# A sparse graph network's set-up: adjacency tiles fetched at once, keys spread by identity matmuls, three ranks on ScalarE, projections and slots spaced anew

## The chip, the cores and the metric

The kernel runs on one core of one Trainium2 chip. A core has TensorE (PE; its weight loads are PEld), VectorE (DVE), ScalarE (ACT), GpSimd (POOL) and SyncE (SP, which here only issues DMAs). Each engine takes its own instructions in the order in which the program has them and waits on semaphores for the others. Times are microseconds of the device (us), from one launch of the whole kernel.

## The reference

Four layers of graph network run one after another on 16 graphs of 1024 nodes with 128 features, which all share one adjacency matrix; each of its entries is 1 with a chance of 0.0078125, about 8 neighbours a node. Layers 0, 2 and 3 are attention layers with 8 heads, layer 1 has one additive score for each pair of nodes.

```python
def _L0_gnn_ref(adj_matrix, h, Wq, Wk, Wv, Wo, ...):   # layers 2 and 3 are the same
    Q = (h @ Wq).reshape(B, N, NUM_HEADS, HEAD_DIM)
    K = (h @ Wk).reshape(B, N, NUM_HEADS, HEAD_DIM)
    V = (h @ Wv).reshape(B, N, NUM_HEADS, HEAD_DIM)
    scores = jnp.einsum('bnhd,bmhd->bhnm', Q, K) / jnp.sqrt(...)
    scores = jnp.where(mask, -jnp.inf, scores)          # mask: adj_matrix == 0
    attn = jax.nn.softmax(scores, axis=-1)
    attn_out = jnp.einsum('bhnm,bmhd->bnhd', attn, V).reshape(B, N, OUT_DIM)
    x = _layer_norm(h + (attn_out @ Wo + bo), ln1_g, ln1_b)
    y = jax.nn.relu(x @ W1 + b1) @ W2 + b2
    return _layer_norm(x + y, ln2_g, ln2_b)

x = L0(adj, x); x = L1(x, adj); x = L2(adj, x); x = L3(adj, x)
```

## The kernel before, in words

The kernel does not multiply by the dense mask. It finds each node's neighbours once, and then fetches only the neighbours' rows of keys and values from tables in DRAM by indirect DMA.

**Set-up, `graph` (L227).** It counts the degree of each node (L256, one count over a 128 x 1024 tile of the adjacency for each of T = 8 tiles), makes a key from degree and node number (L298), and ranks the nodes by it: the keys are spread over all partitions as a 128 x 1024 block in PSUM (`over_partitions`, L282: transpose on PE, copy on DVE, eight matmuls against the selector `sel`), and each rank is the count of keys that are greater (L302, eight compares on DVE). From the ranks come one-hot rows (`perm`, L335), whose matmuls (L344) put node numbers into sorted order (L354). With those, the adjacency rows are gathered again in sorted order (`by_position`, L362, on POOL's queue) into the three buffers `edges`, and for each of eight groups of rows DVE finds the neighbours with MAX8 and MATCH_REPLACE8 (L395 to L403) and writes them to `lists`.

**Slots, `slots` (L408).** For each unit of 128 sorted nodes the lists are spread by PE (L413, `spread`), and some thirty small DVE instructions (L427 to L463) turn them into row indices `idx` and 0/1 matrices `marks`. Unit 0's come at the room "slots" of the set-up, those of the others during the first seven units.

**The first projections, `at_once` (L810).** Eight times, for 128 nodes of the first eight graphs: an x tile is loaded (L816), transposed on PE (L646) and copied by ACT (L652), multiplied by the weights of keys and values (L576), copied by ACT (L580) and written to the table of layer 0 by SP (L585). One such projection is four steps of a generator. What `graph` yields says how many steps are taken there: a number is that many steps, a string calls for something else ("load", "spread", "queries", "slots"; L1128 to L1144). So the yields fix where the projections stand between the other instructions of PE, ACT and SP. The projections of the other eight graphs, `at_leisure` (L787), run later between the parts of the first units.

**The body (L1160 to L1227).** There are 64 units: 4 layers, 2 groups of 8 graphs, 8 tiles of nodes. A unit is a handful of parts of two neighbour rows for each node. A part is gathered on POOL's queue (`gathered`, L929, four buffers `e` of the pool `gathers`, four parts ahead), multiplied by the queries `qr` (L958), reduced to scores (L981), put through the exponential (ACT, L985), weighted (L1009) and summed over neighbours by matmuls against `marks` (L1025). Between the parts, `others` (L1099) takes steps of the tails of the unit before (output projection, norms, feed-forward), of the fronts (the next slots and queries) and of the projections at leisure, one front step to a call.

The order is written out by hand (`manual_schedule`): each engine runs its instructions as the generators emit them. The four gather buffers `wide` serve as scratch in the set-up and are zeroed by POOL (L240, L248, L1155), because rows that a bounds check leaves out keep what was there.

## Time and profile before

| | us |
|---|---|
| median of three timed runs | 2261.7 |
| lowest and highest of them | 2255.61, 2262.03 |
| the profiled execution, whole | 2254.23 |
| its span, first to last instruction | 2251.9 |
| PE busy in the span | 2043.1 |
| DVE busy | 1872.9 |
| ACT busy | 1528.3 |
| POOL busy | 1016.3 |

How to read it: the span is one execution taken by the hardware's profiler, and the times further on are counted from its start. A timeline lists the instructions of one engine with start, duration, line, operation, what is written and read with its size, how often, and in square brackets the idle time just before with what ended it. "DMA to landing" is the time from a DMA's issue until its data is there. The granted TensorE clock is 0.962 of full speed on the mean.

Three more lines of the timelines place ACT and POOL in the set-up. The first two are the copies that begin the second and third projection; the last shows how POOL zeroes three gather buffers.

```profile
17.08 1.07 ACT L652 COPY xT<-ps 128x512 f32<-128x512 f32 x2
...
21.97 1.07 ACT L652 COPY xT<-ps 128x512 f32<-128x512 f32 x2
```

```profile
8.95 10.66 POOL L248 MEMSET e<- 128x4128 f32 x3
```

### The profile page before, as it was taken

Reading aid. Unit: us, or ns where it says so; the run is one execution under the profiler, and the core shown is the slowest. Engines: PE = TensorE matmul, PEld = TensorE weight load, DVE = VectorE, ACT = ScalarE, POOL = GpSimd, SP = SyncE. Lnnn points to the kernel's source line nnn. Section 1 sums busy time; section 2 is a strip of 40 time slices with the busy share of each in tenths; the row PEclk is TensorE's granted clock in tenths of the full one; section 3 lists DMA queues with packets and bytes.
Section 4 is the critical chain, followed back from the end, with each engine's and each line's share of the span. In section 5 each row is a group of like instructions: output and inputs, shape, how many; then the busy total and the mean of one; then the engine's idle time right before and its main releaser. Section 6 shows DMA issues by size and latency. Waiting matters only on the chain.

```text
span 2251.9 us, 36507 instructions
## 1 busy us (share of the span) xinstructions
PE 2043.1 (91%) x13140; PEld 1271.3 (56%) x13140; DVE 1872.9 (83%) x1472; ACT 1528.3 (68%) x5041; POOL 1016.3 (45%) x699
## 2 busy tenths in 40 slices
PE   6589999899999999998999989999999998998986
PEld 5456665555555555554556655656655555555554
DVE  7897899888887577768988889989798998888893
ACT  3346777777777655555677777777777777676765
POOL 3343445354435368884343434334444544453540
PEclk8799999999999999999999999999999998999999
DMA  7897877778788699997997978887888788687860
GB/s 254 290 323 275 298 272 279 268 263 289 284 296 272 221 341 356 360 358 291 327 329 268 318 260 302 303 313 276 284 282 305 265 286 279 225 279 271 288 227 21
DMA packets 164700, 636.05 MB, mean 282 GB/s; under 512 B 34568, under 2 KB 37384, under 8 KB 116014
## 3 DMA queue, kind: packets, MB, share of 16 engines
q0 software_dynamic: 88720, 485.08, 61.0%
q1 hardware_dynamic: 75792, 148.57, 19.1%
q8 instruction: 105, 1.72, 0.3%
q14 instruction: 83, 0.68, 0.1%
HBM read 581.08 MB, written 92.34 MB: 299 GB/s over the span
## 4 chain that ended last, share of the span: by engine, by line
PE 41%; ACT 18%; issue 16%; DVE 11%; DMA 9%; POOL 5%; POOLq 0%; DVEq 0%; ACTq 0%
PE acc L1025 9%; DMA e<-table,idx 8%; PE yps L746 5%; PE ps L576 4%; POOL e L946 4%; PE ps L646 4%; ACT qr L912 4%; PE ps L732 3%; PE ps L909 3%; DVE pr L958 3%; ACT z L624 3%; DVE sc L981 3%; DVE pr L1009 2%; PE yps L750 2%; ACT z L639 2%
## 5 line engine op out<-in xcount | busy, mean ns | idle before, releaser
L946 POOL DMA_INDIRECT e<-table,idx x576 | 854.1, 1483 | 1101.8 <-DVE pr L1009 902.1
L1009 DVE TENSOR_TENSOR pr<-e,ex 128x2048 f32<-128x2048 f32 (+1 forms) x320 | 661.6, 2076 | 46.7 <-ACT ex L985 24.9
L958 DVE TENSOR_TENSOR pr<-e,qr 128x2048 f32<-128x2048 f32 x192 | 441.6, 2300 | 132.7 <-PE acc L1025 55.7
L1025 PE MATMUL acc<-pr,marks 128*32 128x512 f32 x2624 | 519.1, 608 | 14.8 <-DVE pr L1009 10.8
L981 DVE TENSOR_REDUCE sc<-pr 128x128 f32<-128x2048 f32 (+1 forms) x240 | 497.5, 2073 | 8.0
L624 ACT ACTIVATE z<-yps,root 128x128 f32<-128x128 f32 x888 | 317.5, 388 | 35.7 <-PE yps L765 17.2
L1025 PEld LDWEIGHTS acc<-pr,marks 128*32 128x32 f32 x2624 | 107.7, 110 | 269.4 <-issue 226.7
L639 ACT ACTIVATE z<-yps,rstd 128x128 f32<-128x128 f32 x888 | 254.0, 369 | 7.2
L746 PE MATMUL yps<-W,f 128*128 128x128 f32 x1520 | 251.8, 283 | 7.3 <-ACT f L741 1.8
L741 ACT ACTIVATE f<-ps,b 128x512 f32<-128x512 f32 x190 | 129.8, 695 | 157.6 <-PE ps L732 157.2
L746 PEld LDWEIGHTS yps<-W,f 128*128 128x128 f32 x1520 | 205.0, 192 | 51.0 <-issue 25.6
L576 PE MATMUL ps<-Wkv,xT 128*128 128x256 f32 x768 | 215.0, 419 | 20.0 <-ACT xT L652 16.7
L912 ACT COPY qr<-ps 128x512 f32<-128x512 f32 x384 | 197.3, 600 | 40.6 <-PE ps L909 40.5
L909 PE MATMUL ps<-q,rep 32*128 32x512 f32 x768 | 175.3, 661 | 34.7 <-ACT q L904 33.5
L732 PE MATMUL ps<-x,W 128*128 128x512 f32 x384 | 190.4, 620 | 12.5 <-ACT x L654 12.5
L624 ACT ACTIVATION_READ_ACCUMULATOR z<-yps,root 128x1 f32 x888 | 201.7, 227 | 0.0
L646 PE MATMUL ps<-ident,z 128*128 128x128 f32 x896 | 177.5, 299 | 25.5 <-ACT z L639 20.7
L646 PEld LDWEIGHTS ps<-ident,z 128*128 128x128 f32 x896 | 115.2, 142 | 149.2 <-ACT z L639 72.1
L580 ACT COPY kv<-ps 128x512 f32<-128x512 f32 x176 | 103.2, 589 | 131.9 <-PE ps L576 119.4
L576 PEld LDWEIGHTS ps<-Wkv,xT 128*128 128x128 f32 x768 | 146.5, 205 | 76.4 <-ACT xT L652 21.1
L721 PE MATMUL yps<-Wo,oT 128*128 128x128 f32 x768 | 160.3, 292 | 8.6 <-ACT oT L652 8.5
L722 PE MATMUL yps<-centre,x 128*128 128x128 f32 x768 | 155.5, 285 | 3.6
(176 smaller groups left out, 2597.7 us busy)
## 6 DMA issues: line engine op xcount, KB each, us to landing
table<-kv SPq DMA_DIRECT2D x88, 512.0 KB, 6.5
kept<-xT SPq DMA_DIRECT2D x96, 256.0 KB, 5.4
x<-kept SPq DMA_DIRECT2D x48, 512.0 KB, 9.2
qx<-qr SPq DMA_DIRECT2D x48, 256.0 KB, 6.7
e<-table,idx POOLq DMA_INDIRECT x576, 8.1
table<-kv SPq DMA_DIRECT2D x32, 256.0 KB, 7.7
qx<-qr SPq DMA_DIRECT2D x18, 384.0 KB, 9.1
qx<-qr SPq DMA_DIRECT2D x42, 128.0 KB, 8.1
```

Source lines behind the costliest of these rows:

```text
L576: nc.tensor.matmul(ps[:, k, :], x[:, i + k, :], w[LAYERS[l][0], "Wkv"], start=True, stop=True,)
L624: nc.scalar.activation(z[:, i, :], y[:, i, :], AF.Square, scale=D**-0.5, bias=root, accum_out=total[:, i : i + 1],)
L639: nc.scalar.activation(z[:, i, :], y[:, i, :], AF.Copy, scale=rstd[:, i : i + 1])
L646: nc.tensor.transpose(ps[:, i, :], z[:, i, :], ident)
L732: nc.tensor.matmul(ps, p["W1"][:, f * P : (f + 1) * P], x1.rearrange("p g n -> p (g n)"), start=True, stop=True,)
L746: nc.tensor.matmul(ps[:, i, :], f1[:, f, i * P : (i + 1) * P], p["W2"][:, f, :], start=(f == 0), stop=False,)
L912: nc.scalar.copy(qs[u][:, j, h * GH * D : (h + 1) * GH * D], pss[j])
L946: nc.gpsimd.indirect_dma_start(out=es[i][:, k, :], out_offset=None, in_=tables[l, g][:, :], in_offset=bass.IndirectOffsetOnAxis(ap=idx[:, ...
L958: nc.vector.tensor_tensor(prs[i][0][:, :n, :], es[i][:, :n, :ROW], qx[u].rearrange("p (o c) -> p o c", o=1) if (MIX, 0) in piece else of_p ...
L981: nc.vector.tensor_reduce(sc[:, :n, :], prs[i][0][:, :n, :].rearrange("p k (a d) -> p k a d", d=HD), mybir.AxisListType.X, ALU.add,)
L1009: nc.vector.tensor_tensor(prs[i][k0 // 2][:, :m, :].rearrange("p k (a d) -> p k a d", d=d), es[i][:, k0 : k0 + m, base : base + ROW].rearr ...
L1025: nc.tensor.matmul(outs[32 * j : 32 * j + 32], marks[:, mark, :], rhss, start=(chunk == mine[0]), stop=(chunk == mine[-1]),)
```

## The change

- All eight adjacency tiles are fetched first, straight into the empty gather buffers `wide[0]` and `wide[2]`, instead of three at a time through `edges`. The buffers are zeroed afterwards: `wide[0]` by POOL, `wide[2]` by a copy on ACT; of `wide[1]` only the last columns are zeroed.
- `over_partitions` has no transpose, no copy and no selector: a column of the key, repeated 128 times, is the stationary operand of a matmul with the identity.
- Of the eight compares for the ranks, three become `Sign` activations with a sum on ACT (the sum s gives the rank as (s + 1023) / 2), five stay on DVE.
- The steps of `at_once` are taken elsewhere: none during the degree counts, five and two more around the ranks, one at every second one-hot row, six after the sorted nodes, three at each MAX8.
- `slots` has one more empty step between the spread and the DVE work of units 1 to 7, so five steps a unit are handed to the fronts instead of four.

```diff
+SIGNS = 3
...
-        ahead = [by_columns(t) for t in range(3)]
+        held = [wide[k][:, m * N : (m + 1) * N].bitcast(I32) for k in (0, 2) for m in range(T // 2)]
+        for t in range(T):
+            nc.sync.dma_start(held[t], a["adj"][t * P : (t + 1) * P, :])
         yield 0
...
-        junk = wide[1][:, :N]
-        sel = wide[1][:T, N : 2 * N].rearrange("k (t n) -> k t n", n=P)
-
-        nc.gpsimd.memset(wide[1], 0.0)
+        junk, other = wide[1][:, :N], wide[1][:, N : 2 * N]
...
-        for e in wide[3:] + wide[:1] + wide[2:3]:
-            nc.gpsimd.memset(e, 0.0)
+        nc.gpsimd.memset(wide[1][:, 3 * N :], 0.0)
...
             nc.vector.tensor_scalar(
-                junk, ahead[t], 0.0, 0.0, ALU.not_equal, ALU.add, accum_out=deg[:, t : t + 1]
-            )
-            if t + 3 < T:
-                ahead.append(by_columns(t + 3))
-            if t == 4:
+                junk, held[t], 0.0, 0.0, ALU.not_equal, ALU.add, accum_out=deg[:, t : t + 1]
+            )
+            if t == 0:
...
-            yield 1 + t // 4
+            yield 0
...
-            ps = bank([T, P])
-            nc.tensor.transpose(ps, col, ident)
-            turn = s1.tile([T, P], F32, tag="turn", name="turn")
-            nc.vector.tensor_copy(turn, ps)
             dst = accs.tile([P, HF, GH * D], F32, tag="acc", name="acc")
             dst = dst.rearrange("p h d -> p (h d)")
             for t in range(T):
                 nc.tensor.matmul(
-                    dst[:, t * P : (t + 1) * P], sel[:, t, :], turn, start=True, stop=True
+                    dst[:, t * P : (t + 1) * P], col[:, t : t + 1].to_broadcast([P, P]), ident,
+                    start=True, stop=True,
                 )
...
-        for t in range(T):
+        ahead_of = s1.tile([P, T], F32, name="ahead_of")
+        nc.vector.tensor_scalar(ahead_of, key, -1.0, None, ALU.mult)
+        nc.gpsimd.memset(wide[0], 0.0)
+        for t in range(T - SIGNS, T):
+            nc.scalar.activation(
+                other, keys, AF.Sign, bias=ahead_of[:, t : t + 1], accum_out=rank[:, t : t + 1]
+            )
+        nc.scalar.copy(wide[2], seen[:, 0, :1].to_broadcast(list(wide[2].shape)))
+        for t in range(T - SIGNS):
             nc.vector.tensor_scalar(
                 junk, keys, key[:, t : t + 1], 0.0, ALU.is_gt, ALU.add,
                 accum_out=rank[:, t : t + 1],
             )
             yield 1
+        yield 2
+        nc.vector.tensor_scalar(
+            rank[:, T - SIGNS :], rank[:, T - SIGNS :], 0.5, (N - 1) / 2, ALU.mult, ALU.add
+        )
...
                 spread = over_partitions(pack)
                 nc.scalar.copy(values, spread)
-            yield 0
+            yield t % 2
...
         nc.vector.tensor_tensor(bad, bad, low, ALU.add)
-        yield 2
+        yield 6
...
                     nc.vector.match_replace(v, lists[:, q, k : k + 8], last, 0.0)
-                yield 1
+                yield 3
...
             if q:
+                yield
                 yield
                 yield
...
-        fronts.extend([islice(rest, 4), second] + more)
+        fronts.extend([islice(rest, 5), second] + more)
...
-                        fronts.append(islice(rest, 4))
+                        fronts.append(islice(rest, 5))
```

More of the change, by code (lines that the diff above doesn't have):

```diff
@@ L227, in graph @@
     def graph(wide):
-        def by_columns(t):
-            return fetch_edges(
-                lambda e: nc.sync.dma_start(e, a["adj"][t * P : (t + 1) * P, :])
-            )
-        ahead = [by_columns(t) for t in range(3)]
+        held = [wide[k][:, m * N : (m + 1) * N].bitcast(I32) for k in (0, 2) for m in range(T // 2)]
+        for t in range(T):
+            nc.sync.dma_start(held[t], a["adj"][t * P : (t + 1) * P, :])
         yield 0
         iota, values, vs = wide[3][:, :N], wide[3][:, N : 2 * N], wide[3][:, 2 * N : 4 * N]
-        junk = wide[1][:, :N]
-        sel = wide[1][:T, N : 2 * N].rearrange("k (t n) -> k t n", n=P)
-        nc.gpsimd.memset(wide[1], 0.0)
+        junk, other = wide[1][:, :N], wide[1][:, N : 2 * N]
         whole = wide[1][:, 2 * N : 3 * N].bitcast(I32)
@@ L266, in graph @@
                     nid, cols[:, 1, :], float(P), cols[:, 0, :], ALU.mult, ALU.add
-                )
-                nc.vector.tensor_copy(
-                    sel,
-                    ident[:T, :T].rearrange("k (t o) -> k t o", o=1).to_broadcast([T, T, P]),
                 )
```

## The prediction

> **What bounds the kernel now.** I read the page first, then the timelines of the engines over the first 140 us, because `graph`, `slots` and `at_once` run only there, and last the waits between 100 and 480 us, where the spaced slots act.
>
> ```profile
> PE   6589999899999999998999989999999998998986
> ...
> DVE  7897899888887577768988889989798998888893
> ACT  3346777777777655555677777777777777676765
> ...
> PEclk8799999999999999999999999999999998999999
> ```
>
> Each digit is a slice of 56 us. PE is at nine tenths almost everywhere except the first two slices. So the long body is bound by PE; a change to the set-up can only move the body as a whole, earlier or later, by the time at which the first gathers start.
>
> What sets that time is VectorE's chain (DVE; start, duration, then idle before and its releaser):
>
> ```profile
> 12.68 1.22 DVE L256 TENSOR_SCALAR_CACHE_REDUCE e<-edges 128x1024 f32<-128x1024 int32 x1
> ...
> 30.44 0.16 DVE L298 SCALAR_TENSOR_TENSOR key<-deg,nid 128x8 f32<-128x8 f32 x1
> ...
> 35.34 1.28 DVE L302 TENSOR_SCALAR_CACHE_REDUCE e<-acc,key 128x1024 f32<-128x1024 f32 x1 [3.94 <-PE acc L291]
> ...
> 48.31 0.75 DVE L335 TENSOR_SCALAR perm<-e,rank 128x1024 bf16<-128x1024 f32 x1
> ...
> 55.04 0.18 DVE L354 COPY sorted<-ps 128x24 f32<-128x24 f32 x1 [0.47 <-PE ps L344]
> ...
> 61.60 1.23 DVE L395 SCALAR_TENSOR_TENSOR e<-edges,e 128x1024 f32<-128x1024 int32 x1 [2.78 <-DMA edges<-in_adj,node_i]
> ...
> 88.96 0.18 DVE L449 TENSOR_SCALAR idx<-little 128x24 int32<-128x24 int32 x1
> ...
> 98.86 2.29 DVE L958 TENSOR_TENSOR pr<-e,qr 128x2048 f32<-128x2048 f32 x1 [0.67 <-DMA e<-table,idx]
> ```
>
> The reader is to see the milestones: degrees from 12.68, the key at 30.44, first rank 35.34, first one-hot row (`perm`) 48.31, the sorted nodes at 55.04, the first list at 61.60 (after waiting for the gathered adjacency rows), the indices of unit 0 at 88.96 + 0.18, the first product at 98.86. Beside it runs the table of layer 0, which the first gather also reads:
>
> ```profile
> 61.75 0.51 SPq L585 DMA_DIRECT2D table<-qx  x1
> ...
> 82.66 0.51 SPq L585 DMA_DIRECT2D table<-qx  x1
> ```
>
> ```profile
> 55.92 1.12 POOL L363 DMA_INDIRECT edges<-in_adj,node_i  x1 [36.32 <-DVE node_i L359]
> ...
> 89.48 1.01 POOL L946 DMA_INDIRECT e<-table,idx  x1 [4.06 <-DVE little L452]
> 90.79 1.95 POOL L946 DMA_INDIRECT e<-table,idx  x1 [0.30 <-issue]
> ```
>
> The last table write is issued at 82.66, and the first row gather at 89.48 is released by DVE. So the two paths end close together: lists at 89.1, table within some 6 us of 83.2 (landings of table writes: 3.4/6.9/12.1 us least, median, most). DMA over the same stretch, by windows (the last two numbers: DMA share, GB/s):
>
> ```profile
> 15.00:30.00 15.00, 10.73 (x56) 8.81 (x54) 8.89 (x20) 8.08 (x15) 4.61 (x2) 1.00 1.01 354
> ...
> 42.00:50.00 8.00, 5.85 (x39) 4.52 (x37) 7.05 (x18) 4.41 (x8) 0.00 (x0) 1.00 0.92 314
> ...
> 62.00:76.00 14.00, 6.59 (x32) 5.33 (x32) 13.65 (x15) 5.20 (x10) 3.06 (x4) 0.85 0.80 281
> 76.00:90.00 14.00, 10.42 (x52) 7.66 (x56) 13.38 (x29) 5.58 (x10) 4.02 (x5) 0.79 0.77 248
> ```
>
> A full share (1.01) is 354 GB/s here.
>
> **What the Trainium skill says.** "TensorE: Matmul & The Clock Gate", section Step-by-step: matmuls stay in program order and only weight loads are pulled ahead. The trace agrees: at 69.1 PE stands 8.4 us (77.52) for a loaded x, with the last four projections behind it. "ScalarE: Activation LUTs", section What ACT_TABLE_LOAD costs: an activation with a bias pointer takes about 280 ns + 0.833 ns an element. The trace agrees: L624 at 128 elements is 388 ns, the copy L350 of 1024 is 1.01 us. "SBUF — State Buffer", section SBUF: two separate sides: VectorE's two-port modes and GpSimd lock each other out for whole instructions. It agrees: four small `rep` copies took 10.73 us beside POOL's MEMSETs, and the degree count at 12.68 took its usual 1.22 us beside them. "DMA: Bandwidth & Descriptors", section Specifications, gives about 358 GB/s from HBM for a core; the 354 above is that.
>
> **The change, step by step.**
>
> *Degrees.* Before, only three adjacency tiles were in flight: DVE waited 1.10 + 2.46 + 2.48 = 6.0 us for tiles, and did not start before 12.68 because of the locked copies. Now eight tiles (4.2 MB, 12 us at 354 GB/s, so all by about 15) go out first. POOL's early work shrinks from four MEMSETs of 3.53 us to one of 1056 columns (about 0.9 by width) and ends near 6.5. DVE takes tile 0 when it lands (0.76 + 5.5 = 6.3), 1.26 us; the small ops (L155 to L278) about 3.2; seven more counts 8.8; key at about 20.2 against 30.44: **10 us earlier**. The first three x tiles are now issued behind the adjacency, at no cost since no projection starts before 32. The MEMSET of `wide[0]` (3.53) waits on POOL for the counts and has nothing before 50 queued behind it.
>
> *Keys.* Transpose, copy and matmuls were 35.34 − 30.60 = 4.7 us; without the first two (0.8), on a PE that has done nothing before: about 4.2. Ranks begin near 24.6.
>
> *Ranks.* DVE does 5 × 1.33 = 6.7 instead of 10.6. ScalarE's three: 280 + 0.833 × 1024 = 1.13 us, plus 0.23 for the accumulator (L624's row), less overlap: 3.7 in all, hidden beside DVE. The correction of the three costs 0.2. The seven small steps stay at 2.35. First one-hot: 24.6 + 6.7 + 0.2 + 2.35 = 33.9 against 48.31: **14.4 us earlier** on DVE, and the last by 39.4 (no `turn` copy in between).
>
> *What takes its place.* ScalarE must do the signs (to 28.4) and then the new copy into all 4128 columns of `wide[2]`: 0.2 + 4128 × 0.83 = 3.6 us, so it is free at 32. Before, projections began at 10.2; three of eight were done before the key. Now none runs before 32, and the order of PE's instructions in the changed program puts projections 0 and 1 (`at_once`) ahead of the first one-hot's matmuls. One projection is 4.89 us (L652 begins 17.08, next 21.97); the first after a pause 5.6 to 6.8 (56.05 to 61.63; 36.43 to 43.27), I take 6. PE reaches the one-hot at 32 + 6 + 4.3 = 42.3, though DVE had it at 34. Then: first one-hot 0.4, spread of `pack` 2.6 (second L291), three one-hots 0.75, projection 2's transposes 1.0, two one-hots 0.5, four Wkv behind ScalarE's copies 1.1, two one-hots 0.5, 0.4 to the reader: 49.5 against 55.04. So **of 14.4 us, 5.5 are left at the sorted nodes**.
>
> *Lists.* The first adjacency gather took 5.6 us in a stretch where DMA had little else. Now the table writes of projection 2 (2 × 512 KB) and an x tile go out at the same time: 5.6 to 7.5; I take 7. Later gathers have 11 us and more from issue to use (63.09 for 76.78), so they stay hidden. From the first list to indices 27.5 us, unchanged; gathers start at 50.3 + 7 + 27.5 + 0.3 = 85.1 against 89.48.
>
> *Table.* Projection 3 begins (L652) at 52.5, the eighth at 72.1, its copies end at 77.1, issue 77.6. By bytes: 7.3 MB of table, 1.6 of x tiles, 4.2 of lists and 1 of x between 42 and 83 = 14.1 MB, 40 us at 354 GB/s: DMA is full. Landing 6 to 9 us: 84 to 87. So both paths end at about 85.5: **4 us gained** (bounds: 10 if ScalarE's copy and PE's order cost nothing, −2 if writes land as late as their 12.1). Queries end about 77 + 10, before the product at 94.8.
>
> *Slots.* One more step before each of seven slots puts the scores' reduction (2.29) ahead of the slot's work. It is DVE's wait for the spread that this covers:
>
> ```profile
> DVE little L427 <- PE ps L413: 16.6, 5, 6.8
> ```
>
> 16.6 us in five waits, of which up to 5 × 2.2 can be filled. But the chain of waits from 130 to 260 runs over PE and ACT, so I count 1 us of 11. Against it, the next unit's queries come one step later (one wait of 3.1 us for `qr` at 144.5 may become 5): −2 to +3 for the whole, I take −1. At-leisure projections move later by a few steps; the last was issued at 249.5, far before unit 8.
>
> Sum: −4 − 1 = **−5 us**. The profiled execution took 2254.2 (span 2251.9 and 2.3 around it): 2249. The median of the three timed is 2261.7, but one was 2255.6, and the four executions average 2258.4; the time off the profile must be carried to runs like all of these, so 2258.4 − 5 = **2254** in round numbers. About 0.3% (6.8 us) is the least that can be told from no change.
>
> **Rivals.**
> 1. *The front's gain survives whole.* If PE got to the one-hots at 34 (ScalarE's fill cheaper, projections faster), sorted nodes come at 41 and the lists allow gathers at 77; the table (8 × 4.89 from 32, plus 5) still needs 77 + 6. Gain 7 to 10, about 2249. Against: PE's order.
> 2. *Given back to DMA and the body.* The full DMA lands the table near 89, or qr's later wait eats the rest: 2258 to 2260. For: the 40 us of bytes in 41 us. Against: the list gathers travel in a queue of their own.
> 3. *The table becomes the bound, slower.* One mechanism: projections start at 32 instead of 10 and run one behind another. Gathers start at 32 + 1 + 5.5 + 8p + 8, p the period of one. At p = 5.4 this passes 89.5; at the 6.84 seen on a slow PE clock (projection 3 before, clock 0.57 in 30 to 42) it is 101, +12 us: 2270. Against: PE is then nearly without pauses, which kept p at 4.89.
> That the change doesn't do what it says is excluded by the changed program's instructions: three signs, five compares, eight fetches at once, no further table load.
>
> **How the numbers follow.** Forecast (gain 2 to 7) 0.52; rival 1 0.15; rival 2 0.18; rival 3 0.15. Range: from rival 1 with the low end of the timed runs, 2244, up to the middle of rival 3, 2267. Against 2261.7, the line for faster is at 2254.9: the forecast falls below it a little over half of the time (0.28), rival 1 always (0.15), rival 2 seldom (0.02): 0.45. Slower (above 2268.5): most of rival 3 and a tail: 0.15. The rest, 0.40, within 0.3%.
>
> **What would show it.** Key at 20 and first rank near 25; first one-hot on DVE near 34 with DVE then idle some 9 us before the sorted nodes at 49 to 50, and PE idle for ScalarE between 27 and 32: right. First gather at 84 to 87, first product near 95. Wrong if gathers start after 89, if the sign takes more than 1.5 us, or if units 1 to 7 last longer than before (161.8 to 213.7 is unit 1's).

## The result, and the profile after

The kernel after takes 2264.5 us (median of 22 runs, 2254.9 to 2269.2) against 2255.5 for the kernel before in the runs beside it (22, 2246.0 to 2265.8). The ratio is 1.0029, with a 95% interval of 1.0015 to 1.0042 (the means of the two sets differ by 0.3%, their medians by 0.4%): slower by about 0.3%, where faster had been forecast. The profiled execution took 2269.1, its span 2266.9.

Part 2 of the page of the kernel after, the rows that were shown of before (tenths busy in 40 slices):

```profile
PE   5689999899999899998999999999999998998987
...
DVE  5897889788987477778989889888888988888893
ACT  4347677777776555565677776787777767677764
...
PEclk9799999999999999999999999999999998999998
```

In the first slice VectorE is two tenths idler, TensorE one idler and ScalarE one busier; PE shows a few eights where there were nines. Nothing in these rows says where 0.3% went. The timelines say more. VectorE in the kernel after, the milestones of the set-up:

```profile
17.30 0.16 DVE L283 SCALAR_TENSOR_TENSOR key<-deg,nid 128x8 f32<-128x8 f32 x1
...
25.11 1.28 DVE L295 TENSOR_SCALAR_CACHE_REDUCE e<-acc,key 128x1024 f32<-128x1024 f32 x1 [7.44 <-ACT e L290]
...
34.19 5.39 DVE L332 TENSOR_SCALAR perm<-e,rank 128x1024 bf16<-128x1024 f32 x8
47.05 0.18 DVE L351 COPY sorted<-ps 128x24 f32<-128x24 f32 x1 [7.47 <-PE ps L341]
...
53.21 1.23 DVE L392 SCALAR_TENSOR_TENSOR e<-edges,e 128x1024 f32<-128x1024 int32 x1 [1.78 <-ACT qx L578]
...
80.65 0.18 DVE L447 TENSOR_SCALAR idx<-little 128x24 int32<-128x24 int32 x1
...
94.57 2.29 DVE L956 TENSOR_TENSOR pr<-e,qr 128x2048 f32<-128x2048 f32 x1 [4.69 <-DMA e<-table,idx]
```

Every milestone is earlier than before: the key 13 us, the first rank 10, the first one-hot 14, the sorted nodes 8.0, the first list 8.4, the last indices of unit 0 8.3, and the first product 4.3 (94.57 against 98.86). One execution alone would not settle that last figure: in the six traces that this study has of the set-up of before, the first product lies between 94.72 and 102.13, 98.8 on the mean, and in the nine of the set-up of after between 93.83 and 95.41, 94.6 on the mean. The gain is 4.2 us on the means. SyncE's queue and GpSimd's beside it:

```profile
77.05 0.51 SPq L583 DMA_DIRECT2D table<-kv  x1
77.69 0.54 SPq L583 DMA_DIRECT2D table<-qx  x1
```

```profile
86.01 1.00 POOL L944 DMA_INDIRECT e<-table,idx  x1 [8.89 <-issue]
```

The lists were ready at 80.8, yet GpSimd stood 8.89 us, to 86.01: the profile names no releaser ("issue"), but with the indices ready all that a gather still needs is the table, whose last write was issued at 77.69. So I read the table's landing as what now sets the start of the gathers, 8.3 us after that issue. Two traces of the experiments below that hold the landing of the last write bear this out: in e9, which has this set-up, it was issued at 78.04 and landed 7.0 us later, and the first gather went out at 86.03; in e12 it was issued at 78.45, landed 4.4 us later, and the gather went out at 83.92. Both times the gather follows by 1.0 us.

The projections that feed the table do not keep their old pace either, because ScalarE now waits for earlier table writes before it can copy (a line of ScalarE):

```profile
64.10 0.59 ACT L578 COPY kv<-ps 128x512 f32<-128x512 f32 x1 [3.84 <-DMA table<-kv]
```

By windows (span, then busy times, granted clock, DMA share, GB/s), the stretch in which the table is written:

```profile
62.00:76.00 14.00, 11.04 (x56) 8.71 (x55) 13.65 (x15) 6.90 (x14) 4.70 (x5) 1.00 1.04 411
```

The DMA engines are full in it (share 1.04; 0.80 before). What is left of the 4.3 us is soon less: the second product comes at 102.25 against 104.46, and the last instruction group of unit 0, the reciprocal L1060 that I call the end of a unit, at 160.1 against 161.8. By the end of unit 7 the gain is gone: 441.0 against 440.0. The second execution of before (e4 below) has 446.0 there, since its first product came at 102.13 already; the length of units 1 to 7 is steadier, 278.2 and 278.8 us before, 280.8 and 281.4 (e3, the kernel after once more) after.

The wait that the slots' step was to cover, among VectorE's waits between 100 and 480 us (us in all, times, longest):

```profile
DVE little L425 <- PE ps L410: 16.2, 5, 4.4
```

Before, this was 16.6, 5, 6.8: the longest is shorter, the sum nearly the same.

### The profile page after: what moved, and what is told of

It reads as the page before. It is cut to its first block, busy times and chain, and to the rows that moved or that the text cites. A ratio compares the mean times of both kernels' runs of the same rounds, so it can differ in the third digit from the quotient of the medians.

```text
span 2266.9 us, 36503 instructions
## 1 busy us (share of the span) xinstructions
PE 2042.2 (90%) x13138; PEld 1270.1 (56%) x13138; DVE 1860.2 (82%) x1465; ACT 1532.4 (68%) x5048; POOL 1014.5 (45%) x697
## 4 chain that ended last, share of the span: by engine, by line
PE 38%; issue 19%; ACT 15%; POOL 8%; DVE 7%; DMA 7%; POOLq 0%; another core or an unknown queue 0%; DVEq 0%; ACTq 0%
PE acc L1023 9%; DMA e<-table,idx 7%; POOL e L944 6%; PE ps L644 4%; PE yps L744 4%; PE ps L574 4%; PE ps L730 3%; ACT qr L910 3%; PE ps L907 3%; DVE pr L956 3%; ACT z L622 2%; DVE sc L979 2%; PE yps L720 2%; PE yps L748 2%; DVE pr L1007 2%
## 5 line engine op out<-in xcount | busy, mean ns | idle before, releaser
L574 PE MATMUL ps<-Wkv,xT 128*128 128x256 f32 x768 | 215.8, 419 | 35.8 <-ACT xT L650 29.6
L644 PE MATMUL ps<-ident,z 128*128 128x128 f32 x896 | 180.0, 300 | 32.8 <-ACT z L637 27.2
L907 PE MATMUL ps<-q,rep 32*128 32x512 f32 x768 | 170.7, 662 | 29.4 <-ACT q L902 28.4
```

What stands on the lines that cost most here:

```text
L574: nc.tensor.matmul(ps[:, k, :], x[:, i + k, :], w[LAYERS[l][0], "Wkv"], start=True, stop=True,)
L644: nc.tensor.transpose(ps[:, i, :], z[:, i, :], ident)
```

## The experiments

Each kernel below ran beside the kernel before on the same chip, and ratios are to that kernel's runs there, with 95% intervals. Most have 13 to 22 executions; e6, e11, e15, e17 and e18 have six.

### The set-up alone, the slots' step alone

e1 is the kernel after with the slots as they were; e2 is the kernel before with the slots' step; e3 and e4 are the two kernels once more.

```diff
 e1, from after                 e2, from before: the reverse
-                yield
-        fronts.extend([islice(rest, 5), second] + more)
+        fronts.extend([islice(rest, 4), second] + more)
-                        fronts.append(islice(rest, 5))
+                        fronts.append(islice(rest, 4))
```

> The changed kernel with the slots spaced as before (two empty steps instead of three, four front steps a unit instead of five); the whole front stays changed. Theory A (the front gains 4 us at the first product, the slots' extra step loses more in units 1 to 6): first product near 94.6, at the end of unit 7 (440.0 before, 441.0 changed) some 4 us ahead of before, whole ratio to before 0.998 (0.996 to 1.000). Theory B (the slots are innocent; the front's new start costs the body): as the whole change, 1.003 (1.0015 to 1.004), near 441 at unit 7. Theory C (both halves cost): about 1.001.

> The kernel before with only the slots' extra step (three empty steps, five front steps a unit). Theory A: first product at 98.9 as before, unit 7 ends near 445, ratio 1.004 (1.002 to 1.006). Theory B: ratio 1.000, unit 7 at 440.

> The changed kernel once more, for how far the milestones of one execution scatter: ratio 1.003; if the 10 us lost between 700 and 780 (end of layer 0) belong to the change they come again; if they are the scatter of one execution, the milestone at the end of layer 0 differs from 738 by several us.

> The kernel before once more, for the scatter: ratio 1.000 within 0.0015; milestones to unit 7 within 2 us of the first profile (440.0), later ones within 8 us.

Measured: e1 0.9991 [0.9979, 1.0003], e2 1.0041 [1.0026, 1.0056], e3 1.0021 [1.0007, 1.0035], e4 1.0003 [0.9989, 1.0017]. So the slots' extra step costs as much as the whole loss or more: 9 us by e2, and by e3 over e1 some 7. The set-up alone gains 2 us by the ratio of e1, but its interval holds 1 too, so this gain is not shown. In e1's trace the first product is at 94.17 and the end of unit 0 at 159.5: the set-up does there what it does in the kernel after. e4 missed one thing that was expected of it: its unit 7 ends 6.0 us from the first profile's, where 2 were allowed for, all of it before the end of unit 0 (167.2 against 161.8).

### Late work, or late fronts?

The step does two things: VectorE's work for the slots comes a step later, and so does all that the hand-written order takes up after the slots (queries, loads of x, projections at leisure). e5 keeps the first and undoes the second; e6 does the second alone.

```diff
 e5, from after                              e6, from after
 at the end of slots' work:                  before the work, and behind it:
-            yield                           -                yield
+            yield "again"                   +            if q:
 in others():                                +                yield
+            if got == "again":
+                continue
```

> The changed kernel, but the step that follows the slots' DVE work is taken in the same call as that work, so the queries, the loads and the projections at leisure are no later than before, while the DVE work of the slots still stands one step later, behind the reduction. Theory A1 (what costs is that everything behind the slots in the fronts comes one step later): as the front alone, ratio 0.999 (0.997 to 1.001), unit 7 near 437, projections at leisure done near 250. Theory A2 (what costs is the slots' DVE work behind the reduction, or the marks and indices coming later): as the whole change, 1.003 (1.0015 to 1.004), unit 7 near 442.

> The changed kernel, but with the additional empty step behind the slots' DVE work instead of ahead of it: the work stands where it stood before, what follows in the fronts comes one step later. Theory A1: ratio 1.003 (1.0015 to 1.004), projections at leisure done near 317. Theory A2: 0.999 (0.997 to 1.001).

Measured: e5 1.0006 [0.9994, 1.0018], e6 1.0065 [1.0041, 1.0090]. Late work alone costs less than the two together, 0.0015 over e1, and it does cover VectorE's wait for the spread (6.3 us in e5), which the two together do not. Late fronts alone cost more than the two together, so the costs don't add up. In e6, VectorE's timeline shows the worst of it, the slots' first copy:

```profile
331.43 0.79 DVE L424 COPY little<-ps 32x24 f32<-32x24 f32 x4 [5.85 <-PE ps L410]
```

VectorE stood 5.85 us for the spread on PE; then PE ran dry in its turn. Windows of e6 (the columns as above: length, PE, PEld, DVE, ACT, POOL, clock, DMA share, GB/s):

```profile
335.00:338.00 3.00, 3.00 (x37) 1.78 (x30) 2.97 (x4) 1.04 (x3) 0.00 (x0) 1.00 0.71 225
338.00:341.00 3.00, 1.44 (x13) 1.25 (x12) 2.93 (x3) 1.31 (x9) 0.95 (x1) 1.00 0.27 93
341.00:344.00 3.00, 2.76 (x12) 1.03 (x12) 2.97 (x4) 2.60 (x9) 1.03 (x2) 0.79 0.63 148
344.00:347.00 3.00, 3.00 (x13) 2.64 (x13) 3.00 (x2) 1.36 (x4) 0.00 (x0) 0.50 0.89 259
347.00:350.00 3.00, 3.00 (x18) 3.00 (x17) 2.97 (x3) 0.97 (x2) 1.32 (x1) 0.57 0.63 254
```

```profile
341.24 0.63 PE L645 MATMUL ps<-ident,o 128*128 128x128 f32 x4 [1.80 <-ACT q L903]
```

PE is busy for 1.44 of 3 us from 338, its longest pause is the 1.80 us before 341.24, and in the next windows its granted clock is 0.79, 0.50 and 0.57. So a wait may cost twice: once as it lasts, and once as a slower clock behind it. The Trainium skill, "TensorE: Matmul & The Clock Gate", section What's actually happening, tells of such a gate: the clock halves after an idle window of about 3.4 us and comes back after a busy one. This trace agrees with the halving, but it had no idle window of that length: the pause was 1.80 us. From 344 to 350 PE was busy without a pause, mostly at about half the clock. That the pause set the halving off is possible; no run took only the pause away.

### Which of the fronts?

First the projections at leisure alone, earlier in the kernel after (e9), later in the kernel before (e10); and e11, e1 with one step taken away from the slots instead of added.

```diff
 e9, from after                             e10, from before
-                eager[0] = 1 if u < 2 else 0  (both)
+                eager[0] = 1 if u < 3 else 0       +  ... 1 if u < 1 else 0
 e11, from e1: slots' empty steps 2 -> 1, both islice(rest, 4) -> islice(rest, 3)
```

> The whole change, but the projections at leisure get their additional step in unit 2 as well (eager for units 0 to 2 instead of 0 and 1). Theory A1a (of what comes later behind the slots, it is the projections at leisure, spilt into units 3 to 5, that cost): they end near 255 instead of 317, unit 7 ends near 438, ratio 0.9995 (0.998 to 1.001). Theory A1b (it is the queries and the loads of the next units that come too late): unit 7 near 441 to 443, ratio 1.002 to 1.003.

> The kernel before, but the projections at leisure get their additional step in unit 0 alone, so that they spill into later units while queries and loads stay. Theory A1a: they end after 300, units 1 to 7 last 3 to 7 us longer than 278, ratio 1.003 (1.001 to 1.006). Theory A1b: ratio 1.000, units 1 to 7 in 278.

> The changed front with one empty step fewer in the slots than before (one instead of two, three front steps a unit). Theory A1 continued to the other side: whatever stands behind the slots comes a step earlier: unit 7 ends 1 to 3 us earlier than with two empty steps (437.3), ratio 0.998. Rival (the spread's matmuls need the distance, DVE waits for them): 1.001 or more.

Measured: e9 1.0021 [1.0005, 1.0037], e10 1.0009 [0.9995, 1.0023], e11 1.0074 [1.0046, 1.0102]. In e9 the last table write of these projections is at 238.9 us (before 249.5, after 316.8), and the loss stays; in e10 it is at 352.5, and its interval holds 1. So the projections' lateness alone isn't it. And e11 shows that "later is worse" is no rule: a step earlier is worse too. There VectorE reaches the slots before the spread and waits 28.6 us in five waits instead of 15.3, 10.3 in one.

Then the loads of x. e15 puts the empty step behind the queries, so that loads and projections alone are late; e16 puts the transposes of unit 1's x tile first (the tile itself is asked for in the set-up already); e17 delays the transposes of the next x tile; e18 takes a step away ahead of them, in the kernel after.

```diff
 e15, from before
                     fronts.append(queries(u + 1))
+                    if u < T - 1:
+                        fronts.append(iter([None]))
 e16, from after
-        fronts.extend([islice(rest, 5), second] + more)
+        fronts.extend([second, islice(rest, 5)] + more)
 e17, from before, in loaded()               e18, from after, in loaded()
+            if u > 1:                                    for h in range(HF):
+                yield "idle"                +                if u < 2 or h:
             for h in range(HF):             +                    yield "idle"
                 yield "idle"                -                yield "idle"
                 yield "idle"                                 yield "idle"
```

> The kernel before, with the empty step behind the queries: only loads and the projections at leisure come a step later, queries and slots' work do not. If the late queries are what costs, the ratio is 0.999 to 1.001; if late loads and projections cost, it is 1.002 to 1.004, with a wait of some 4 us for an x tile near 160 us.

> The kernel after, with unit 1's x tile asked for ahead of the first slots' steps: the one wait of 4.2 us of TensorE for that tile at 160 us goes. If that wait is part of what the extra step costs, the end of unit 0 is 2 to 4 us earlier than 160.1 and the ratio falls from 1.0029 to about 1.0015; if TensorE is only behind by other work there, nothing changes.

> The kernel before, with the transposes of the next x tile one step later in each unit; slots, queries and the projections at leisure keep their steps. If these late transposes are what the empty step costs, the ratio is 1.002 to 1.005; if it is the projections, or all of them together, it is 0.999 to 1.001.

> The kernel after, with the transposes of the next x tile one step earlier, so that they fall where they fell before; slots' work and queries stay a step later. If the late transposes are the cost, the ratio falls from 1.0029 to 0.998 to 1.001; if not, it stays at 1.002 to 1.004.

Measured: e15 1.0087 [1.0063, 1.0110], e16 1.0022 [1.0006, 1.0038], e17 1.0091 [1.0060, 1.0121], e18 1.0163 [1.0135, 1.0190]. e15 leaves slots and queries where they were and is slow. That points to the late loads of x, since late projections alone (e10) showed no cost. In e17 four transposes for each half of an x tile, one step later, cost more than the whole change. But e17 is not the change's step on a smaller scale. Its edit takes hold of the x tiles of units 2 to 15, where the change's step has units 1 to 7. In its profiled execution units 1 to 7 take 280.1 us, 1.9 more than the 278.2 before, and units 9 to 14, which the change leaves alone, are longer each (37.7 to 39.1 us; 36.3 to 36.8 before, 36.5 to 37.6 in e4). And at an "idle" step the projections at leisure take a step too, so theirs now stands ahead of the transposes. e17 shows that late transposes cost in this body, not how much of the change's loss they are. e16 is a miss: PE's wait for an x tile stays (4.5 us), because the tile it waits for is not unit 1's but unit 2's, which GpSimd asks for at 153.05 in the kernel after (144.26 before): in unit 0 the loads no longer get a step of their own before the unit ends. e18 is the other surprise: it is far worse. Its edit does more than was meant. The step that it takes away was also a step of the projections at leisure, whose last table write moves on to 346.4 (after 316.8), and in units 8 to 15 it puts the transposes ahead of where they stood before the change. The loss is in units 1 to 7, 307.3 us against 280.8. PE's and VectorE's waits of e18 between 158 and 455 us:

```profile
PE ps L574 <- ACT xT L650: 14.4, 5, 3.5
...
PE ps L644 <- ACT z L637: 6.0, 6, 1.0
```

```profile
DVE pr L1008 <- ACT ex L984: 20.8, 6, 5.2
DVE little L425 <- PE ps L410: 18.6, 5, 5.8
```

PE now waits 14.4 us for ScalarE's copies `xT` of the projections at leisure (in e1 2.8), up to 3.5 in one, and VectorE 20.8 for ScalarE's exponentials. So e18 does not test the transposes alone, and its miss says nothing against them as a cause.

### What the traces of all of them share

One thing that differs is what PE has between asking ScalarE for something and needing it. The kernel before, PE around 305 us; then the kernel after at the same place:

```profile
304.98 1.92 PE L1025 MATMUL acc<-pr,marks 128*32 128x512 f32 x16
306.83 1.06 PE L646 MATMUL ps<-ident,z 128*128 128x128 f32 x4
307.73 0.60 PE L646 MATMUL ps<-ident,x 128*128 128x128 f32 x4
308.26 1.91 PE L1025 MATMUL acc<-pr,marks 128*32 128x512 f32 x8
310.10 1.98 PE L732 MATMUL ps<-x,W 128*128 128x512 f32 x4
```

```profile
304.35 1.92 PE L1023 MATMUL acc<-pr,marks 128*32 128x512 f32 x16
306.21 0.66 PE L644 MATMUL ps<-ident,xg 128*128 128x128 f32 x4
307.28 1.10 PE L644 MATMUL ps<-ident,z 128*128 128x128 f32 x4 [0.42 <-ACT z L637]
308.23 0.60 PE L644 MATMUL ps<-ident,x 128*128 128x128 f32 x4
309.93 1.13 PE L574 MATMUL ps<-Wkv,xT 128*128 128x256 f32 x4 [1.11 <-ACT xT L650]
310.99 1.91 PE L1023 MATMUL acc<-pr,marks 128*32 128x512 f32 x8
```

Before, the transposes of x (L646, `ps<-ident,x`) are followed by eight matmuls of the weighted sum (L1025), and no step waits. After, the transposes of `z` wait 0.42 for ScalarE, then come x's, then a projection at leisure at once, which waits 1.11 for `xT`; the sum stands behind it. Each is small, and such waits come back four to seven times in this stretch. TensorE's waits of the kernel after, 158 to 455 us:

```profile
PE ps L594 <- ACT xT L652: 7.8, 7, 1.9
PE ps L644 <- ACT z L637: 4.3, 6, 1.0
PE ps L574 <- ACT xT L650: 4.2, 4, 1.1
PE ps L644 <- DMA x<-in_x,places: 4.2, 1, 4.2
```

In e1 the same places have 4.9, 1.0, 2.8, and no line for the last. The table sets the sum of all PE waits between 130 and 450 us, from the one profiled execution, beside the timed ratio; "clock" is the median over the timed executions of the mean granted clock. The last column has the length of units 1 to 7 in the profiled execution, and the granted clock in them.

| kernel | ratio to before | PE waits, us | clock | units 1 to 7, us (clock in them) |
|---|---|---|---|---|
| before; e4 | 1; 1.0003 | 21.5; 21.9 | 0.962 | 278.2 (0.975); 278.8 (0.982) |
| e1, e7, e8 | 0.9991, 0.9994, 0.9995 | 21.6, 21.4, 21.4 | 0.965, 0.966, 0.965 | 277.8 (0.982), 275.8 (0.988), 276.1 (0.988) |
| e12; e13 | 0.9964; 0.9982 | 20.9; 21.5 | 0.970; 0.965 | 276.7 (0.988); 277.3 (0.982) |
| e10 | 1.0009 | 23.5 | 0.962 | 276.6 (0.981) |
| e5 | 1.0006 | 24.6 | 0.963 | 277.8 (0.982) |
| e14 | 1.0002 | 27.0 | 0.964 | 287.6 (0.953) |
| after; e3 | 1.0029; 1.0021 | 29.0; 29.4 | 0.964; 0.963 | 280.8 (0.982); 281.4 (0.979) |
| e2 | 1.0041 | 28.0 | 0.959 | 284.8 (0.967) |
| e9, e16 | 1.0021, 1.0022 | 27.3, 29.6 | 0.964, 0.965 | 280.3 (0.960), 288.4 (0.959) |
| e15, e17 | 1.0087, 1.0091 | 27.3, 27.2 | 0.958, 0.958 | 284.2 (0.988), 280.1 (0.988) |
| e6 | 1.0065 | 32.5 | 0.960 | 294.5 (0.944) |
| e11 | 1.0074 | 26.8 | 0.962 | 292.2 (0.947) |
| e18 | 1.0163 | 36.6 | 0.958 | 307.3 (0.928) |

Without late fronts or late work PE waits 21 to 22 us there; every kernel that is slower than before beyond its interval waits 26.8 or more (e14, which ties with before, has 27.0 and the better set-up). After against e1 it is 7.4 us more, near the size of the loss (0.0038 of 2257 is 8.6). But that is agreement in size and not yet a cause. Units 1 to 7 of the kernel after are only 3.0 us longer than those of e1 (280.8 against 277.8; 3.6 in e3), at nearly the same clock in them, so these traces place about half of the loss or less where the waits are; where the rest is, they don't show. The longest units, those of e6, e11, e14, e16 and e18, have a lower clock as well (0.959 and less); in the kernel after it is 0.982, no lower than before. For e15, e17 and e11 the waits make up about a third of the loss; e15 and e17 have the lowest clock beside e18. The profiled execution of e15 took 2257.5 us with its 27.3 of waits, no more than the median of before beside it (2257.6), while its other five took 2267.8 to 2280.6. In e17's six executions time and clock go together: 2262.0 at 0.962, the profiled one, up to 2286.5 at 0.953. What pulls the clock down in the other five no trace shows, since only one execution of each kernel has one.

### The set-up: what can still be had

Back to the first 100 us. e7 is e1 without the signs (eight compares on VectorE) and with the fill of `wide[2]` on GpSimd; e8 moves the fill alone; e12 has no signs, and its fill on ScalarE behind the copy of the values, with no projection step among the one-hots; e13 is e12 again; e14 is e12 with the slots and the two edits of e5.

```diff
 e8 (e7 too), from e1
-        nc.scalar.copy(wide[2], seen[:, 0, :1].to_broadcast(list(wide[2].shape)))
+        nc.gpsimd.memset(wide[2], 0.0)
 e12, from e1
-        for t in range(T - SIGNS, T):
-            nc.scalar.activation(other, keys, AF.Sign, ...)
-        nc.scalar.copy(wide[2], ...)
-        for t in range(T - SIGNS):
+        for t in range(T):
...
-            yield 1
+            yield int(t < T - SIGNS)
...
                 nc.scalar.copy(values, spread)
+                nc.scalar.copy(wide[2], ...)
-            yield t % 2
+            yield 0
```

> The changed front with the slots as before, but all eight compares on DVE, no signs, and wide[2] zeroed by POOL as wide[0] is: ScalarE is free for the projections as soon as the keys stand. Theory F (the signs and the fill only delay the projections, and PE reaches the one-hots behind them): first projection copy near 21.5 instead of 28.5, PE at the one-hots before DVE (38), sorted nodes near 44 instead of 47, last table write near 71 instead of 77.7, first gather near 78 instead of 86, first product near 87 instead of 94.4, ratio to before 0.995 (0.993 to 0.998). Rival (the signs are worth their place): sorted nodes at 47 or later, first product at 94 or later, ratio 0.999 or more.

> The changed front with the slots as before and the signs kept, but wide[2] zeroed by POOL: only the copy of 3.6 us on ScalarE is gone. Theory F: projections start 3.6 earlier (24.9), sorted nodes near 43.5 to 44, first gather near 82.4, first product near 91, ratio 0.9975 (0.995 to 0.999). Rival (the copy is hidden): first product at 94, ratio 0.999.

> The changed front with slots as before; all eight compares on DVE, the fill of wide[2] on ScalarE after the copy of the packed values, and no projection step between the one-hots. Theory F (the projections' late start and their place between the one-hots held the front): first projection copy near 25, sorted nodes near 41, last table write near 71, first gather near 75, first product near 85 to 87 instead of 94.2, ratio 0.996 (0.994 to 0.998) if the body takes the gain over. Theory G (the body does not take over what the front gains, since unit 0 waits for the same DMA traffic): first product earlier by 8, but unit 7 by less than 4 against 437.3 and ratio 0.999 or more.

> The set-up without signs, the fill of the third wide buffer on ScalarE after the values, the slots in four steps as before, once more. If its gain over the kernel before is real (first product 5 us earlier at 93.7, and nothing in the body changed), the ratio is 0.996 to 0.998 again; if the first measurement had the luck of fewer pauses of TensorE's clock, it is 0.998 to 1.000, as the front alone gave.

> The same set-up, and the slots' work on VectorE behind the reduction without holding up queries and loads. Theory that VectorE's wait for the spread matters: that wait falls from 15.5 to about 6 us and the ratio is 1 to 3 us below that of the same set-up with four steps. Theory that TensorE, which is behind, decides: equal to it within 0.1%.

Measured: e7 0.9994 [0.9982, 1.0007], e8 0.9995 [0.9982, 1.0007], e12 0.9964 [0.9945, 0.9983], e13 0.9982 [0.9968, 0.9996], e14 1.0002 [0.9988, 1.0015]. In e7 and e8 the fill met VectorE. VectorE's timeline in e8, then GpSimd's:

```profile
17.22 3.59 DVE L268 TENSOR_SCALAR three<-deg 128x8 bf16<-128x8 f32 x1
17.30 3.51 DVE L283 SCALAR_TENSOR_TENSOR key<-deg,nid 128x8 f32<-128x8 f32 x1
```

```profile
17.25 3.54 POOL L293 MEMSET e<- 128x4128 f32 x1 [1.51 <-DVE e L250]
```

The conversion to bf16 (L268, 0.18 us in e1) lasted as long as GpSimd's MEMSET, which fits the lock that the prediction cited, and the key was done with it: 3.4 us later on the path. In e12 they don't meet, and the lists begin earlier:

```profile
17.29 0.16 DVE L283 SCALAR_TENSOR_TENSOR key<-deg,nid 128x8 f32<-128x8 f32 x1
21.39 1.28 DVE L288 TENSOR_SCALAR_CACHE_REDUCE e<-acc,key 128x1024 f32<-128x1024 f32 x1 [3.94 <-PE acc L275]
...
34.37 5.38 DVE L322 TENSOR_SCALAR perm<-e,rank 128x1024 bf16<-128x1024 f32 x8
40.32 0.18 DVE L342 COPY sorted<-ps 128x24 f32<-128x24 f32 x1 [0.57 <-PE ps L331]
...
45.95 1.23 DVE L383 SCALAR_TENSOR_TENSOR e<-edges,e 128x1024 f32<-128x1024 int32 x1 [1.85 <-DMA edges<-in_adj,node_i]
...
79.52 0.79 DVE L415 COPY little<-ps 32x24 f32<-32x24 f32 x4 [8.28 <-PE ps L401]
...
93.70 2.29 DVE L946 TENSOR_TENSOR pr<-e,qr 128x2048 f32<-128x2048 f32 x1 [2.71 <-DMA e<-table,idx]
```

The sorted nodes are at 40.32, 6.7 us earlier than in the kernel after, the first list at 45.95. Yet this gain does not reach the gathers. The lists still need the spread on PE, which stands in PE's order behind the last of the first projections, and VectorE waits 8.28 us for it; the last indices of unit 0 come at 81.76, 1.1 us later than in the kernel after. The last table write goes out at 78.45 and the first gather at 83.92. So lists and table both end behind the projections, the table last, and the first product is only 0.9 us earlier (the second 3.4: 98.90 against 102.25). Three traces of this set-up put the first product at 93.70, 96.33 (e13) and 90.49 (e14). e7, e8 and e12 all missed what was expected of it (94.88, 92.68 and 93.70 against 87, 91 and 85 to 87). e12 is the fastest kernel of the study and its repetition agrees within the intervals: by 0.2 to 0.4% it beats the kernel before. A part of it is in the clock (0.970 and 0.965 against 0.964 and 0.962 in the runs beside them), so the set-up is not shown to be the whole of it. e14 is a miss: late slots' work took VectorE's wait for the spread from 15.5 to 6.3 us, as in e5, and PE's waits rose to 27.0 (`q` 9.2 us against 3.4 in e13): 0.2% lost against e13, not gained, at the edge of what the two intervals can part.

## Why the prediction was wrong

**Degrees and key: right in kind, too small.** The key was forecast for 20.2 and came at 17.30. The first count began at 4.35, not at 6.3, because its tile landed sooner; the small operations after it took 2.9 us, not 3.2; and the terms of the sum make 19.6, not 20.2. The rate of the other tiles (418 GB/s from 8 to 12 us, where the sum took 354) did not matter, since VectorE waited for none of them.

**Signs beside the compares: wrong, and it cancelled out.** The three signs took 1.11 + 0.19 each, within 3.7 us, as forecast. But they were to be hidden beside VectorE's compares, and the first rank waits 7.44 us "<-ACT e L290" until the signs are done; without signs (e12) it is at 21.39. So the key's 3 us were lost to the signs, and the first rank's forecast (24.6, came 25.11) was met by two errors of opposite sign. Signs and compares read the same block `acc` and write parts of the same tiles, `wide[1]` and `rank`; which of these made the program order one behind the other was not tried.

**What takes its place: right in kind.** ScalarE's fill took 3.62; the first projection's copy began at 28.50, not 32, but that projection took 7.9 us (28.50 to 36.38) and not 6, so that PE reached the one-hots at 40.57 (42.3). The sorted nodes came at 47.05 (49.5), with VectorE idle 7.47 us before them.

**Lists and table: right that they end close together, right in the sum.** First gather 86.01 against 85.1, first product 94.57 against 94.8. Which path ends last was left open; it is the table. The lists were ready at 80.8, 4 us before the forecast. The table's last write went out at 77.69, as forecast (77.6), by luck: the projections had begun 3.5 us early and then ran at 5.6 us each instead of 4.89, from the fourth (49.38) to the eighth (71.95). The start of the gathers came 8.3 us after that write, where the landing was taken as 6 to 9. A reading beside it was wrong without effect: behind PE's wait that ends at 77.52 in the kernel before stand eight matmuls, half of one projection, not four projections.

**The front's gain at the end: half, or less.** The sum took −4 from the first product. The second product gained only 2.2, since it waits 3.07 us for its rows, and e1 gives 2 us with an interval from a gain of 5 to a loss of 1.

**Slots: the step that failed.** The prediction counted −1 for the slots' extra step, with −2 to +3 as its bounds, from a wait of VectorE that the step would cover and a `qr` that might come later. Measured by e2 the step costs +9, by e3 over e1 +7. The mechanism as put failed too, and not its size alone. The step covers the wait only where the fronts are not made late with it (6.3 us in e5 and e14); in the kernel after it stays (16.6 before, 16.2 after). And covering it gains nothing: e5 and e14 come out 0.15 and 0.2% slower than e1 and e13. The sum left out the loads of x, which the empty step pushes back too, and put the projections at leisure at nothing. e15, with only loads and projections late, costs 0.9%, and e10, with only projections late, shows no cost (its interval holds 1). That points to the late loads of x with their transposes on PE, and e17 shows that late transposes can cost. That they do so because PE, which bounds the body, loses the filling between its questions to ScalarE and the answers fits the waits (29.0 us against 21.6 in e1), but it is argued and not shown: no run puts the filling back and nothing else, and in the kernel after units 1 to 7 lengthen by less than the waits. The prediction itself read PE at nine tenths and then costed the edit on VectorE. What stays open is where the rest of the loss lies, why e2, e15 and e17 run at a lower granted clock in most executions, and which place for the transposes would be best together with late slots.

**The range held the time, the sign did not.** That the time lies in the range is luck: its upper end came from rival 3, a table so slow that the gathers start later than before, and they start 3.5 us earlier. The base of the forecast was also high: it took 2261.7 and 2258.4 from four executions, and the 22 beside the kernel after have 2255.5. Rival 2, the gain given back to the body, was nearest in kind, with "qr's later wait" as the cause; `qr` was not it (3.1 us before, 3.5 after). Rival 3's slow projections did come: the last three table writes of projections go out at 66.59, 72.22 and 77.69, a period of 5.5 to 5.6, beyond the 5.4 that the rival named. They had begun at 28.5 and not at 32, and these 3.5 us kept the gathers ahead of 89.5. The last test named, units 1 to 7 longer than before, is what happened: 280.8 us against 278.2 (e3 281.4, e2 284.8; e4 278.8, e1 277.8).

## What to carry to other kernels

An empty step in a hand-written order is not free because the engine it is meant for has room: list all that is queued behind it, and ask of each what it was filling on the engine that bounds. Measure the parts of a change apart before adding them: a set-up worth 0.1% or nothing and a spacing that costs 0.4% looked like one change of 0.3%. An edit that moves one thing in such an order seldom moves it alone: e17 and e18 also moved steps of the projections, and acted in more units than the change. When one of two paths that end together is shortened, look for what both still wait for: in e12 the lists began 7 us earlier, but their last step and the table both stood behind the same projections, and the first product moved by 0.9.

## What the runs showed of the hardware

The granted clock differs between executions of one and the same program, and in one place two forms of it go with two clocks. From unit 9 on, the four executions compared here run the same body. The lengths of units 9 to 16, from the ends of units, are, in us:

| | 9 | 10 | 11 | 12 | 13 | 14 | 15 | 16 |
|---|---|---|---|---|---|---|---|---|
| before | 36.8 | 36.5 | 36.4 | 36.6 | 36.7 | 36.3 | 27.8 | 35.8 |
| e12 | 36.8 | 36.5 | 36.4 | 36.6 | 36.7 | 36.3 | 27.8 | 35.8 |
| before again, e4 | 37.6 | 36.5 | 36.5 | 36.5 | 36.8 | 37.2 | 32.0 | 35.3 |
| e1 | 38.0 | 36.1 | 36.6 | 36.4 | 36.7 | 37.3 | 30.6 | 39.4 |

Two agree to the tenth, and the kernel before differs from itself by 5.5 us (282.9 and 288.4 in sum). By windows, units 15 and 16 with the end of unit 14, in e1 and then in e12:

```profile
690.00:733.40 43.40, 37.53 (x269) 24.83 (x268) 28.79 (x23) 29.25 (x117) 21.15 (x19) 0.96 0.79 254
733.40:772.90 39.50, 35.55 (x208) 20.34 (x208) 15.37 (x19) 19.88 (x78) 11.26 (x12) 0.91 0.63 199
```

```profile
685.90:724.50 38.60, 34.61 (x263) 22.62 (x263) 28.98 (x24) 28.23 (x114) 22.80 (x18) 1.00 0.83 270
724.50:760.30 35.80, 33.52 (x214) 19.66 (x214) 15.37 (x19) 20.85 (x82) 12.04 (x13) 1.00 0.71 237
```

The longer form has a clock of 0.96 and 0.91 where the other has 1.00. What causes which no run shows. Its 8 us in e1 are as much as all that this study is about, and the reason why single profiles of these kernels can't be compared by their spans.

The DMA engines moved more than the prediction had taken for full: 418 GB/s between 8 and 12 us and 411 between 62 and 76 in the kernel after, at shares of 1.03 and 1.04, where the kernel before shows 354 at 1.01. "DMA: Bandwidth & Descriptors", section Measured, has up to 425 for large loads by one core with its neighbour idle, which these windows bear out; the figure of 358, of the section that the prediction cited, was the wrong one for this kernel.
